# A four-layer graph attention kernel: which sources a target tile takes whole, and how many gather buffers it has

## The chip, the cores and the metric

The kernel runs on one core of one Trainium2 chip, in one launch. The metric is device time in microseconds (us). Three runs of the kernel before gave a median of 1810.38 us, from 1797.26 to 1814.76; the execution that the profile shows took 1796.08 us, and its span from the first to the last instruction is 1794.3 us. The engines are called as the profile calls them: PE multiplies matrices (PEld is its weight load), DVE works on vectors, ACT evaluates functions, POOL (GpSimd) here mostly issues gathers, and SP issues the other transfers.

## The reference

`x` is 4096 x 256 in float32 and `adj` is 4096 x 4096 with entries 0 and 1. An edge between nodes i and j is drawn with a probability proportional to 1/sqrt((1+i)(1+j)), so nodes with a low number are hubs and most of the matrix is zero. Four layers follow each other, each of the form `x = x + attention(relu(layernorm(x)), adj)`:

```python
h = jnp.maximum(_layernorm(x, axis=-1), 0.0)
g = h @ W                                      # projection
e = leaky_relu((g @ a1)[:, None] + (g @ a2)[None, :], 0.2)
att = softmax(where(adj > 0, e, -large), axis=1)
x = x + act(att @ g)
...
```

Layer 0 has one head of 256 and a bias, layer 1 one head and an elu at the end, layer 2 four heads of 64, and layer 3 two attentions over the same mask (the softmax of e and of -e), each with a projection of its own, and an elu. A row of `adj` is a target, a column is a source: each target sums over the sources it has an edge to.

## The kernel before, in words

**Tiles and steps.** The 4096 nodes are 32 tiles of 128, and 8 blocks of four tiles. A *step* is the work of one source tile for a unit of targets. DVE forms the weights `s_p` (the exponential of the leaky relu is a maximum of two products, times the mask; L1032), and PE multiplies them with the sources' projected rows and adds into PSUM (L1068 for layers 0, 1 and 3; L1093 for layer 2, with the operands the other way round). ACT makes the weights of two of the four heads of layer 2 (L1018) before DVE multiplies them with the mask (L1041).

**Two kinds of units.** A *dense* unit holds a block of four target tiles and goes over all 32 source tiles. `DENSE = (4, 2, 1, 1)` blocks are treated so in layers 0 to 3. All other target tiles are *listed*, each a unit of its own: it takes the first `DP` source tiles whole, and of the rest only those sources that have an edge to at least one of its 128 targets. These are gathered, 128 rows at a time, by an indirect transfer on POOL (`s_gg`, L1228) from a table of projected rows in memory, through a list of indices `idx_T`. `CAPS[T]` is the number of such gathers of target tile T. A listed tile therefore has `DP + CAPS[T]` steps. Where the lists do not fit into `CAPS`, a flag is set and a dense version of all layers runs afterwards. Before, `DP` is 4.

**Where whole sources lie.** The projected rows of the first `DP` tiles stay on chip (`L.pre`), and so do their masks (`mpre`). The rows of the other tiles go to the table, and dense units of layers 1 to 3 read them back in chunks of four tiles (`s_gs`, with the mask chunk `s_ms`) on the SP queue, three chunk buffers deep. In layer 0 all projected rows stay on chip (`g`).

**The lists and masks.** During layer 0 the adjacency is loaded in int32, turned into bytes (L1322), written to memory chunk by chunk (L1324), and reduced to "which source has an edge to this tile" (`seen`, L1329). `list_sources` turns that into indices: prefix sums, one-hot matrices on DVE (L875) and 28 small matmuls per target tile on PE (L900). The byte masks of the listed sources are gathered as well (`mlist`, L928), once, and kept for all layers; those of target tiles 4 to 15 come along with a layer's first gathers and are copied to `mlist` by ACT (L1240).

**Order.** Instructions of POOL stay in the order in which the program writes them; the other engines' order comes from a scheduler. `run` fetches a step six steps before it is multiplied, so a gather's place on POOL is fixed there. In layer 0 one or two listed steps follow each dense step from dense step 40 on, and one mask gather is issued per dense step. In layer 1, 16 dense steps stand alone at the start and the other 48 are spread over 24 listed tiles; in layer 2, 36 of 128 (one per head and source tile) stand alone and the rest is spread over 14 of 28 tiles; in layer 3, 16 of 64 stand alone and the rest is spread over 28 tiles. Gathers of a layer can start when all its table rows are written. In layers 1 to 3 the gathers share a pool of 9 buffers (`gat`), so POOL is at most 9 gathers ahead of the steps that use them; layer 0 has its own 7.

Of the kernel before, what the change touches and what calls it, by code (L numbers as in the profile page):

```python
# [9 lines left out]
F16 = mybir.dt.float16  # L10
# [7 lines left out]
P = 128  # L18
# [434 lines left out]

DP = CH
JT = NT - DP
TS0 = IT
DENSE = (4, 2, 1, 1)

ORDER = (None, (0, 4, 1, 5, 2, 6, 3, 7), (0, 4, 5, 6, 7, 2, 1, 3), (0, 2, 3, 4, 5, 6, 7, 1))
LISTED0 = 40
CAPS = (25, 17, 15, 13, 12, 11, 11, 10, 10, 9, 9, 9, 8, 8, 8, 8) + (8,) + (7,) * 7 + (6,) * 8
MAXCAP = max(CAPS[TS0:])
OFFS = [sum(CAPS[TS0:T]) for T in range(NT + 1)]
NLIST = OFFS[NT]
# [13 lines left out]
def list_layers(ctx: ExitStack, tc: tile.TileContext, a: dict, out: bass.AP, flag):  # L480
# [305 lines left out]

    def list_constants(pool):

        place = pool.tile([P, P, JT // 2], F16, name="place")
        nc.gpsimd.iota(  # L790
            place, pattern=[[1, P], [0, JT // 2]], base=0, channel_multiplier=0, allow_small_or_imprecise_dtypes=True
        )
        lists = pool.tile([P, MAXCAP, JT * IT], F16, name="lists")
        nc.gpsimd.iota(
            lists,
            pattern=[[1, MAXCAP], [0, JT * IT]],
            base=0,
            channel_multiplier=0,
            allow_small_or_imprecise_dtypes=True,
        )  # L800

        code = pool.tile([P, JT * IT], F16, name="code")
        n = (NT // 2 - DP) * IT
        for part, tiles, base in ((code[:, 0:n], NT // 2 - DP, DP * P - HALF), (code[:, n:], NT // 2, 1)):
            nc.gpsimd.iota(
                part,
                pattern=[[CH * P, tiles // CH], [1, CH], [0, IT]],
                base=base,
                channel_multiplier=CH,
                allow_small_or_imprecise_dtypes=True,  # L810
            )
        sums = []
        for k in range(2):
            t = pool.tile([P, NT // 2 + JT, IT], F32, name=f"sums_{k}")
            nc.gpsimd.memset(t[:, 0 : NT // 2, :], 0.0)
            sums.append(t)
        return place, lists, code, sums

    def list_sources(ib, seen, pool, consts):

        n = JT * IT
        place, lists, code, sums = consts
        half = JT // 2
        used = pool.tile([P, JT, IT], F16, name=f"used_{ib}", tag="used")
        nc.vector.tensor_scalar(used, seen, 0.0, None, op0=ALU.is_gt)
        yield 4.0
# [44 lines left out]

        def one_hot(T, j):

            first = pool.tile([P, P, half], F16, name=f"first_{T}_{j}", tag="first", bufs=2)
            nc.vector.tensor_tensor(  # L875
                first,
                place,
                lof[:, T % IT, j : j + half].unsqueeze(1).to_broadcast([P, P, half]),
                op=ALU.is_equal,
            )  # L880
            return first


        ahead = [(ib * IT + t, j) for t in range(IT) for j in (0, half)]
        firsts = [one_hot(*ahead[0])]
        yield 4.0
        for t in range(IT):
            T = ib * IT + t
            cap = CAPS[T]
            ps = None  # L890
            for j in range(JT):
                if j % half == 0:
                    first = firsts.pop()
                    ahead.pop(0)
                    if ahead:
                        firsts.append(one_hot(*ahead[0]))
                    yield
                if ps is None:
                    ps = ps_mm.tile([P, MAXCAP], F32, name=f"idx_ps_{T}", tag="mm")
                nc.tensor.matmul(  # L900
                    ps[:, 0:cap],
                    lhsT=first[:, :, j % half],
                    rhs=val[:, 0:cap, j * IT + t],
                    start=(j == 0),
                    stop=(j == JT - 1),
                )
                if j % 7 == 6:
                    yield
            idx = keep.tile([P, cap], I32, name=f"idx_{T}", tag=f"idx_{T}")
            nc.vector.tensor_scalar(idx, ps[:, 0:cap], float(HALF), None, op0=ALU.add)  # L910
            index[T] = idx
            yield
# [278 lines left out]
    def run(plan):  # L1191

        n = len(plan)
        for p in range(n + LEAD[3]):
            if p + 4 < n and plan[p + 4][1] == 0 and plan[p + 4][0].is_ready():
                plan[p + 4][0].prepare()
            for lead, stage in zip(LEAD, (Unit.fetch, Unit.begin, Unit.weigh, Unit.multiply)):
                if 0 <= p - lead < n:
                    stage(*plan[p - lead])
            if p >= LEAD[3]:  # L1200
                u = plan[p - LEAD[3]][0]
                clock[0] += u.cost
                pump(posts, u.rates[0], width=2)
                pump(lists_q, u.rates[1])
                gather_masks(u.rates[2])


    def listed_sources(L, T, pool):
# [36 lines left out]
    with ExitStack() as phase:  # L1245
# [65 lines left out]
        def mask_chunk(ib, c):  # L1311

            load()
            if ib == 0:
                behind(c)
            m = (
                mpre[:, :, ib * IB : (ib + 1) * IB]
                if c == 0
                else mpool.tile([P, CH, IB], U8, name=f"s_m_{ib}_{c}", tag="m")
            )  # L1320
            for h, raw in enumerate(loaded[ib, c]):
                nc.vector.tensor_scalar(m[:, h * half : (h + 1) * half, :], raw, 0.0, None, op0=ALU.is_gt)  # L1322
            if c > 0 or ib in MASKS_IN:
                nc.sync.dma_start(mask_rows(ib, c * CH), m)  # L1324
            if ib > 0:
                if c == 0:
                    seen[ib] = lists_p.tile([P, JT, IT], F32, name=f"seen_{ib}", tag="seen", bufs=4)
                else:
                    nc.vector.tensor_reduce(  # L1329
                        seen[ib][:, (c - 1) * CH : c * CH, :].rearrange("p j t -> p (j t)"),  # L1330
                        m.rearrange("p j i -> p (j i)")
                        .bitcast(I32)
                        .rearrange("p (t w) -> p t w", w=P // 4),
                        AX.X,
                        ALU.max,
                    )
                if c == NCH - 1:
                    push(lists_q, list_sources(ib, seen[ib], lists_p, consts))
            return m
# [52 lines left out]


    late = ctx.enter_context(tc.tile_pool(name="s_late", bufs=1))
    gat = ctx.enter_context(tc.tile_pool(name="s_gather", bufs=9))
    stream = ctx.enter_context(tc.tile_pool(name="s_stream", bufs=3))
    for l in (2, 3):
        L = weights(l, late, late, nc.sync)
# [11 lines left out]
    for l in (1, 2, 3):  # L1410
        L = layers[l]

        def all_sources(L, T0, nt, heads, per):


            held = {}
            n = L.part
            cols = slice(heads[0] * n, (heads[-1] + 1) * n)
            w = slice(T0 * P, (T0 + nt) * P)

            def get(i):
                jt, k = divmod(i, per)
                jt = ORDER[L.l][jt // CH] * CH + jt % CH
                mine = heads[k : k + 1] if per > 1 else heads
                if jt < DP:
                    ensure(lambda: L.ready[jt])
                    return mine, [L.pre[:, jt, h * n : (h + 1) * n] for h in mine], mpre[:, jt, w]
                if jt % CH == 0 and k == 0:
                    ensure(lambda: all(L.ready[jt : jt + CH]))
                    gt = stream.tile(  # L1430
# [112 lines left out]
```

## Time and profile before

| | before |
|---|---|
| median of 3 runs | 1810.38 us |
| span of the profiled execution | 1794.3 us |
| ACT busy | 631.0 us (35%) |
| gathers of rows `s_gg` / of masks `mlist` | 715 / 105 |
| layer 0 ends (last addition to x, L1122) | 520.6 us |
| layer 1 ends (L1140) | 852.0 us |
| layer 2 ends (L1160) | 1370.0 us |
| layer 3 ends (L1182) | 1783.3 us |

Each float32 matmul stands in the records as two instructions (1430 of them for the 715 gathered steps of one matmul each), and a group's busy time, not its mean, counts what it really occupied. [...] Idle time of an engine counts only in a stage in which another engine waits for it. For POOL, idle time that ends with a PE or DVE instruction is a wait for a free buffer; a gap of 0.30 us, put down to "issue" or to whatever semaphore came last, stands ahead of every gather.

### The profile page before, as it was taken

To read this page: it belongs to the slowest core of one execution; us is meant where nothing else is said; L and a number is where in the kernel's file an instruction comes from. 1 tells how busy PE (TensorE), PEld (TensorE's weight loads), DVE (VectorE), ACT (ScalarE), POOL (GpSimd) and SP (SyncE) were. 2 spreads that over 40 slices of the span, in tenths; PEclk is the share of its full clock that TensorE was granted. 3 is DMA by queue.
4 is the path that set the end of the run, shared out by engine and by line. 5 is a ranking of instruction groups with operands and counts; after the bars stand their busy time and mean duration, and the time that the engine had idled before them with its cause. 6 is when DMAs were issued, how large, how long until landed. Compare 5 with 4: busy or idle time off the path is not lost.

```text
span 1794.3 us, 29158 instructions
## 1 busy us (share of the span) xinstructions
PE 1660.2 (93%) x9268; PEld 1384.3 (77%) x9268; DVE 1319.1 (74%) x3908; ACT 631.0 (35%) x1915; POOL 960.5 (54%) x930
## 2 busy tenths in 40 slices
PE   6998899799889999888999999988889999999997
PEld 4886777678778778676577878788888888888876
DVE  6787899777744676556788888877785566777755
ACT  5630010020120232333467666788884011111101
POOL 8836666646535656553353444444561666655453
PEclk9999999999879999989999999999999999999999
DMA  7888778853244444543233332323342665666553
GB/s 258 301 299 281 242 244 251 264 143 110 60 135 138 134 117 134 147 132 106 82 94 86 90 90 81 98 82 83 99 116 75 197 208 175 183 180 178 160 165 107
DMA packets 152237, 274.70 MB, mean 153 GB/s; under 512 B 21423, under 2 KB 75340, under 8 KB 152076
## 3 DMA queue, kind: packets, MB, share of 16 engines
q0 software_dynamic: 45584, 130.39, 26.8%
q1 hardware_dynamic: 105656, 141.83, 24.2%
q8 instruction: 77, 1.26, 0.3%
q14 instruction: 84, 0.69, 0.1%
q10 hardware_dynamic: 836, 0.53, 0.1%
HBM read 231.76 MB, written 40.90 MB: 152 GB/s over the span
## 4 chain that ended last, share of the span: by engine, by line
PE 78%; DVE 8%; issue 4%; DMA 3%; POOL 3%; ACT 2%; another core or an unknown queue 2%; SPq 0%; POOLq 0%; DVEq 0%; ACTq 0%
PE s_acc L1068 44%; PE s_accm L1093 20%; PE s_pj L748 8%; DVE s_p L1032 3%; PE idx_ps L900 2%; PE s_tp L716 2%; PE s_sT L966 2%; DMA s_gg<-table,idx 1%; DMA s_raw<-in_adjT 1%; ACT s_p L1018 1%; DVE s_m L1322 1%; POOL s_z L702 1%; POOL s_gg L1228 1%; DVE s_p L1041 0%
## 5 line engine op out<-in xcount | busy, mean ns | idle before, releaser
L1228 POOL DMA_INDIRECT s_gg<-table,idx x715 | 757.9, 1060 | 733.5 <-PE s_acc L1068 228.6
L1032 DVE SCALAR_TENSOR_TENSOR s_p<-s_grow,s_gg,mlist 128x128 f32<-128x128 f32 x994 | 310.1, 346 | 143.0 <-PE s_acc L1068 85.9
L1068 PE MATMUL s_acc<-s_gg,s_p 128*128 128x257 f32 x1430 | 353.8, 390 | 9.9 <-DVE s_p L1032 7.8
L1068 PEld LDWEIGHTS s_acc<-s_gg,s_p 128*128 128x128 f32 x1430 | 270.5, 194 | 53.6 <-DVE s_p L1032 12.6
L1068 PE MATMUL s_acc<-g,s_p 128*128 128x257 f32 x1152 | 292.5, 397 | 14.2 <-DVE s_p L1032 5.3
L1068 PEld LDWEIGHTS s_acc<-g,s_p 128*128 128x128 f32 x1152 | 220.0, 198 | 49.7 <-issue 12.3
L1032 DVE SCALAR_TENSOR_TENSOR s_p<-s_grow,pre,mpre 128x128 f32<-128x128 f32 (+1 forms) x576 | 189.2, 369 | 49.4 <-PE s_acc L1068 30.5
L1093 PE MATMUL s_accm<-s_p,s_gg 128*65 128x128 f32 x1744 | 204.7, 273 | 1.7 <-issue 1.6
L1068 PE MATMUL s_acc<-s_gs,s_p 128*128 128x257 f32 x896 | 203.6, 380 | 0.0
L1032 DVE SCALAR_TENSOR_TENSOR s_p<-s_grow,s_gs,s_ms 128x512 f32<-128x512 f32 x224 | 161.9, 748 | 50.7 <-PE s_accm L1093 24.7
L748 PE MATMUL s_pj<-s_w,s_hT 128*128 128x259 f32 (+3 forms) x640 | 175.9, 417 | 24.9 <-ACT s_hT L718 9.5
L1093 PEld LDWEIGHTS s_accm<-s_p,s_gg 128*65 128x65 f32 x1744 | 193.2, 138 | 5.3 <-issue 2.8
L1018 ACT ACTIVATE s_p<-s_grow,s_minus,s_gg 128x128 f32<-128x128 f32 x436 | 186.7, 485 | 25.9 <-PE s_accm L1093 15.0
L1068 PE MATMUL s_acc<-pre,s_p 128*128 128x257 f32 x768 | 184.0, 384 | 5.5 <-ACT s_y L1179 3.5
L1068 PEld LDWEIGHTS s_acc<-s_gs,s_p 128*128 128x128 f32 x896 | 169.4, 190 | 24.7 <-issue 0.6
L972 ACT ACTIVATE s_grow<-s_sT 128x256 f32<-128x256 f32 (+2 forms) x136 | 46.8, 367 | 379.3 <-PE s_sT L966 260.9
L748 PEld LDWEIGHTS s_pj<-s_w,s_hT 128*128 128x128 f32 x640 | 126.3, 205 | 56.4 <-ACT s_hT L718 14.2
L1068 PEld LDWEIGHTS s_acc<-pre,s_p 128*128 128x128 f32 x768 | 144.5, 192 | 28.4 <-ACT s_y L1179 3.9
L928 POOL DMA_INDIRECT mlist<-mask_t,idx x105 | 122.1, 1162 | 65.1 <-issue 30.0
L1093 PE MATMUL s_accm<-s_p,pre 128*65 128x128 f32 (+1 forms) x928 | 122.2, 286 | 2.6 <-issue 2.5
L1093 PEld LDWEIGHTS s_accm<-s_p,pre 128*65 128x65 f32 x928 | 105.1, 139 | 21.0 <-issue 18.3
L1018 ACT ACTIVATE s_p<-s_grow,s_minus,pre 128x128 f32<-128x128 f32 x224 | 95.0, 485 | 23.2 <-issue 18.9
(126 smaller groups left out, 1743.5 us busy)
## 6 DMA issues: line engine op xcount, KB each, us to landing
s_raw<-in_adjT SPq DMA_DIRECT2D x128, 512.0 KB
s_gs<-table SPq DMA_DIRECT2D x28, 516.0 KB
s_gg<-table,idx POOLq DMA_INDIRECT x715
mask_t<-s_m SPq DMA_DIRECT2D x35, 256.0 KB
table<-s_g SPq DMA_DIRECT2D x28, 258.0 KB
s_ms<-mask_t SPq DMA_DIRECT2D x28, 256.0 KB
table<-s_m SPq DMA_DIRECT2D x21, 256.0 KB
table<-g SPq DMA_DIRECT2D x8, 516.0 KB
```

Of the source, the lines that this page charges most:

```text
L702: (nc.gpsimd if L.l == 0 else nc.vector).tensor_scalar(z, x[:, T, :], mv[:, k, 0:1], 0.0, op0=ALU.subtract, op1=ALU.max)
L716: nc.tensor.transpose(tp[:, c, :], zs[k][:, c * P : (c + 1) * P], ident)
L748: nc.tensor.matmul(ps, lhsT=hT[:, c, :], rhs=L.w[:, c, k * (D + 6) : k * (D + 6) + cols], start=(c == 0), stop=(c == 1),)
L900: nc.tensor.matmul(ps[:, 0:cap], lhsT=first[:, :, j % half], rhs=val[:, 0:cap, j * IT + t], start=(j == 0), stop=(j == JT - 1),)
L928: nc.gpsimd.indirect_dma_start(out=mlist[:, OFFS[T] + k, :], out_offset=None, in_=mask_t[T // IT], in_offset=bass.IndirectOffsetOnAxis(ap= ...
L966: nc.tensor.transpose(ps[:, h - h0, it, :], L.s[:, T0 + it, h : h + 1].to_broadcast([P, P]), ident)
L972: nc.scalar.activation(grow[:, h1:h2, :], ps[:, h1 - h0 : h2 - h0].rearrange("p h a b -> p h (a b)"), AF.Exp, scale=scale,)
L1018: nc.scalar.activation(w[:, h, :], u.grow[:, h, :], AF.Relu, scale=g[h][:, n - 1 : n], bias=minus)
L1032: nc.vector.scalar_tensor_tensor(p[:, k, :], u.grow[:, h, :], g[k][:, n - 1 : n], m, op0=ALU.min if L.l == 3 and h == 1 else ALU.max, op1= ...
L1068: nc.tensor.matmul(u.accs[it][h], lhsT=p[:, k, it * P : (it + 1) * P], rhs=g[k][:, 0:n], start=first, stop=last,)
L1093: nc.tensor.matmul(u.regions[h], lhsT=g[k][:, 0 : DH + 1], rhs=p[:, k, :],  start=first and (u.nt > 1 or h == 0), stop=last, skip_group_ch ...
L1228: nc.gpsimd.indirect_dma_start(out=wide, out_offset=None, in_=L.table, in_offset=bass.IndirectOffsetOnAxis(ap=index[T][:, k : k + 1], axis=0),
```

## The change

Only source tile 0 is still taken whole; tiles 1 to 3 join the lists. A source tile taken whole costs a step, whether its sources have edges to these 128 targets or not; a listed one costs only its share of the gathered rows. So `DP` falls from 4 to 1 and `CAPS` rises, and every listed tile has one or two steps fewer and one to three gathers more. `JT`, the number of listed source tiles, goes from 28 to 31, an odd number, so the one-hot matrices come in halves of 16 and 15 tiles. The first chunk of source tiles is now treated as all others: its mask is written to memory and reduced, and its rows and mask are read back by the dense units of layers 1 to 3. The on-chip copies `L.pre` and `mpre` shrink to a quarter, and the room goes to 17 gather buffers in place of 9. In layer 0, every fourth dense step issues two mask gathers instead of one.

```diff
-DP = CH
+DP = 1
 JT = NT - DP
+HALFT = (JT + 1) // 2
...
-CAPS = (25, 17, 15, 13, 12, 11, 11, 10, 10, 9, 9, 9, 8, 8, 8, 8) + (8,) + (7,) * 7 + (6,) * 8
+CAPS = (28, 20, 17, 16, 14, 13, 13, 12, 12, 11, 11) + (10,) * 4 + (9,) * 5 + (8,) * 8 + (7,) * 4
...
-                gather_masks(u.rates[2])
+                gather_masks(u.rates[2] and u.rates[2] + (plan[p - LEAD[3]][1] % 4 == 3))
...
-            m = (
-                mpre[:, :, ib * IB : (ib + 1) * IB]
-                if c == 0
-                else mpool.tile([P, CH, IB], U8, name=f"s_m_{ib}_{c}", tag="m")
-            )
+            m = mpool.tile([P, CH, IB], U8, name=f"s_m_{ib}_{c}", tag="m")
...
-            if c > 0 or ib in MASKS_IN:
-                nc.sync.dma_start(mask_rows(ib, c * CH), m)
+            nc.sync.dma_start(mask_rows(ib, c * CH), m)
             if ib > 0:
                 if c == 0:
                     seen[ib] = lists_p.tile([P, JT, IT], F32, name=f"seen_{ib}", tag="seen", bufs=4)
-                else:
-                    nc.vector.tensor_reduce(
...
+                    nc.scalar.copy(mpre[:, :, ib * IB : (ib + 1) * IB], m[:, 0:DP, :])
+                j0 = DP if c == 0 else 0
+                nc.vector.tensor_reduce(
...
-    gat = ctx.enter_context(tc.tile_pool(name="s_gather", bufs=9))
+    gat = ctx.enter_context(tc.tile_pool(name="s_gather", bufs=17))
...
-                if jt < DP:
-                    ensure(lambda: L.ready[jt])
-                    return mine, [L.pre[:, jt, h * n : (h + 1) * n] for h in mine], mpre[:, jt, w]
                 if jt % CH == 0 and k == 0:
```

## The prediction

> **What bounds the kernel now.** I read the page first, then the busy time of each engine in stretches that follow the layers, then POOL's waits, then single gathers in time order.
>
> ```profile
> PE 1660.2 (93%) x9268; PEld 1384.3 (77%) x9268; DVE 1319.1 (74%) x3908; ACT 631.0 (35%) x1915; POOL 960.5 (54%) x930
> ...
> L1228 POOL DMA_INDIRECT s_gg<-table,idx x715 | 757.9, 1060 | 733.5 <-PE s_acc L1068 228.6
> ```
>
> PE looks like the bound and POOL half idle. By stretch (layer 0 to 537; layer 1 to 852, its target tiles 16 to 31 to 716, then 8 to 15; layer 2 to 1390; then layer 3), each column being busy us with the number of instructions:
>
> ```profile
> core 0: us, PE busy (x) PEld busy (x) DVE busy (x) ACT busy (x) POOL busy (x), PEclk, DMA share, GB/s
> 121.00:235.00 114.00, 98.09 (x575) 80.81 (x573) 96.65 (x229) 11.05 (x40) 80.58 (x64) 0.98 0.85 270
> ...
> 537.00:716.00 179.00, 167.58 (x786) 141.01 (x785) 114.61 (x362) 39.99 (x143) 105.78 (x105) 0.99 0.46 130
> 716.00:852.00 136.00, 116.37 (x484) 92.04 (x483) 79.53 (x238) 43.45 (x158) 68.10 (x69) 0.92 0.45 129
> 852.00:1146.00 294.00, 289.22 (x1839) 213.37 (x1838) 255.94 (x748) 187.89 (x498) 131.93 (x121) 0.99 0.32 87
> 1146.00:1390.00 244.00, 222.13 (x1726) 206.79 (x1725) 186.69 (x638) 189.68 (x557) 101.51 (x99) 0.99 0.33 93
> 1390.00:1707.00 317.00, 316.00 (x1479) 274.76 (x1478) 218.91 (x706) 38.27 (x98) 189.45 (x180) 1.00 0.62 183
> ```
>
> The first part of layer 2 and most of layer 3 are PE's almost without a gap (289 of 294, 316 of 317); the second part of layer 2 has PE at 222 of 244. Layers 0 and 1 are not: PE has 6 to 14% of idle time, and no other engine is full either. POOL's own rhythm, in layer 3:
>
> ```profile
> 1570.16 0.95 POOL L1228 DMA_INDIRECT s_gg<-table,idx  x1 [0.30 <-PE s_acc L1068]
> 1571.41 0.95 POOL L1228 DMA_INDIRECT s_gg<-table,idx  x1 [0.30 <-PE s_acc L1068]
> ...
> 1581.76 1.34 POOL L1228 DMA_INDIRECT s_gg<-table,idx  x1 [4.38 <-PE s_acc L1068]
> ```
>
> A gather costs POOL 0.95 us plus a gap of 0.30 us which no view counts as busy. So the price is a *pitch*: mean busy plus 0.30. From the stretches: layer 0, 80.58/64 = 1.26, so 1.56 in the one shown, and 1.45 over the whole layer from 121 on (213 instructions, 244.2 us); layer 1, 105.78/105 and 68.10/69, so 1.30; layer 2, 1.39 and 1.33; layer 3, 1.35. With that, POOL is occupied for 180 x 1.35 = 243 of 317 us in layer 3, not 189, and the waits of 4.38 us are its slack: a free buffer, released by PE.
>
> For PE's price of a step I take runs in the chain of waits:
>
> ```profile
> 41.92 3.04 PE s_acc L1068 x14
> ...
> 966.37 2.62 PE s_accm L1093 x24
> ```
>
> Seven matmuls of 257 columns in 3.04 us are 0.434 each; twelve of layer 2 in 2.62 are 0.218 each, 0.873 for a step of four heads.
>
> [...]
>
> **The change, part by part.** Steps of listed tiles, from the sums of CAPS: layer 0 (tiles 16 to 31) 169 to 144, layer 1 (8 to 31) 270 to 235, layers 2 and 3 (4 to 31) 330 to 291 each. Gathers of rows: 105 to 128, 174 to 211, 218 to 263, 218 to 263, together 150 more; mask gathers 105 to 128. Counting sources with the reference's inputs, all lists fit, so the dense fallback stays out.
>
> PE loses 25 x 0.434 = 10.9 us in layer 0, 35 x 0.434 = 15.2 in layer 1, 39 x 0.873 = 34.1 in layer 2, 78 x 0.434 = 33.9 in layer 3 (two attentions). It gains 28 x 3 = 84 list matmuls at 0.07 (14 take 0.98 us), 5.9 us, in layer 0. Net 88 us less.
>
> DVE loses 216 weights of 346 ns and 39 of 417, 91 us, of which only 8.7 in layer 0. There it gains nearly 15 us: the one-hots (60.8 us) grow by 124/112, the two list products (11.8 us) by 1736/1344, and seven more reductions take at most 0.68 each. ACT loses 78 x 0.485 = 38 us and gains 22 mask copies (6.4) and seven copies of one mask tile (at most 0.6 each: a copy of 512 columns takes 577 ns); layer 2's weights hide them. SP writes five more mask chunks of 256 KB in layer 0, against 67 MB of adjacency: nothing that the 0.85 DMA share there would show.
>
> POOL gains 173 gathers, about 235 us. What that means, by layer:
>
> Layer 0. From the first mask gather (121.0) to the last row gather (514.4) are 393 us, of which 210 x 1.45 = 305 are occupied. After: 256 x 1.45 = 371. It fits, with 22 us to spare in a queue in fixed order, where a gather that waits for an index or a buffer holds up all behind it, and PE's listed steps after those. PE's tail after the last dense step gets shorter (33 listed steps were left at 470; the order of the changed kernel leaves about 15). Between -15 and +30; I take +5.
>
> Layer 1. Rows are gathered from 537 on. 211 x 1.30 = 274, so the last is issued at 811 at the earliest; add 6 for waits and the 23 that lie between the last gather (829.3) and the end now: 840 against 852, -12. PE alone would allow -15, and more if 17 buffers close the bubbles of tiles 8 to 15, but POOL's sum does not.
>
> Layer 2. POOL needs 135 x 1.39 = 188 of 294 us and 128 x 1.33 = 170 of 244. It stays below PE, so PE's 34.1 come through: -33.
>
> Layer 3. POOL: 263 x 1.345 = 354 from 1390, 1744; plus 4 for waits and the 22 from the last gather (1772.6) to the end: 1770 against 1794, -24. PE alone would allow -34. The 17 buffers matter here: they let POOL use the 16 dense steps at the start (28 us) to get 17 gathers ahead, 23 us of the 28; with 9, it would have had 12.
>
> The added wait: each of the five dense units of layers 1 to 3 now loads chunk 0, where it had `pre` on chip. At the start of layer 1 that load waits on SP for the last gathers of layer 0; behind it on SP are the mask chunk, later chunks and the last row stores. PE first needs it some 5 us later (now transposes and a projection fill 522 to 526). From 0 to 8 us; I take 2, inside layer 1's 6. In layers 2 and 3 chunk 0 has long been written and a chunk buffer is free early, hidden behind the preceding listed tiles.
>
> Sum: 5 - 12 - 33 - 24 = -64 us of 1794.3, 3.6%; on the median of 1810.4, 1746.
>
> **The rivals.** *PE stays the bound everywhere.* For it: POOL's waits for PE releases are 228.6 + 128.4 us, and gathers without interference take 1.25. Then 88 us go, and about 10 more from bubbles in tiles 8 to 15 of layer 1, where ACT waits 61.9 us for gathers to land. Against it: the sums 274 and 354 above. 1712.
>
> *Layer 0 eats the gain.* POOL's queue and DVE (97 of 114 us busy) are both close to full there; +30 in layer 0, -5 in layer 1, -20 and -10 after: 1805, no change.
>
> *POOL's waits don't shrink.* Its time between the first and the last gather of a layer, less the occupied part, is 393 - 305 = 88 us in layer 0, 292 - 226 = 66 in layer 1 and 383 - 293 = 90 in layer 3. If half of that is latency rather than slack, the gathers of layer 0 end at 121 + 371 + 44 = 536 against 514 (+22, and up to +20 more for dense steps that stall behind them), layer 1 at 537 + 274 + 33 + 23 = 867 (+15), and layer 3 at 1390 + 354 + 45 + 22 = 1811 (+17); with -33 in layer 2 that is +41, so 1851, slower. Against it: in layer 3 the waits come once per tile right after seven gathers back to back, which is the picture of a full buffer pool, not of latency.
>
> **How the numbers follow.** POOL takes over layers 1 and 3 (1746): 0.54. PE stays the bound (1712): 0.26. Layer 0 eats the gain (1805): 0.10. Waits stay (1851): 0.10. The range from 1700 to 1790 leaves out the last and most of the third. Faster by over 1% (below 1792): the first two and a fifth of the third, some of the first lost to a larger layer 0, 0.82; within 1%: 0.09; slower: 0.09.
>
> **What would show it.** 865 row gathers with a pitch near 1.3; POOL's waits for PE nearly gone in layers 1 and 3, and PE's share falling from 316 of 317 there; layer 2 shorter by 33 with PE still full; the last layer-0 gather still near 515. The prediction is wrong if POOL's pitch moves (a tenth of a us is 26 us in layer 3 alone), if layer 0 grows by tens of us, or if PE waits for chunk 0 at layer starts.

## The result, and the profile after

The changed kernel took 1899.17 us (median of 4 runs, 1894.10 to 1903.07) against 1803.82 us for the kernel before, measured beside it (4 runs): 1.052 times as long, with an interval of 1.045 to 1.060. I had forecast 1746 us and given slower a chance of 0.09.

One thing about the numbers has to be said first, because it came out of the experiments and runs through all of them. On two chips of the runs below the kernel before takes 1700 us, on four it takes 1782 to 1798 us, and the first measurement resembles these four. I call them 1700-us chips and 1790-us chips. No chip is on record at two times, so it isn't shown whether the difference belongs to the chip itself or to something that held there at that time. Every ratio of the experiments compares runs on one chip.

Page of the changed kernel, first measurement: engines, and the group of row gathers.

```profile
PE 1643.3 (87%) x8764; PEld 1343.3 (71%) x8764; DVE 1263.3 (67%) x3660; ACT 606.9 (32%) x1866; POOL 1141.8 (60%) x1104
...
L1233 POOL DMA_INDIRECT s_gg<-table,idx x865 | 914.5, 1057 | 636.7 <-PE s_acc L1073 187.0
```

There are 865 gathers, and one costs POOL what it did before (mean 1057 ns, before 1060). But POOL, which was to be full, has 637 us of idle time left before them. PE executes 504 instructions fewer and its share falls from 93 to 87%, in a longer span. By stretch (the first is that of before; then layer 1, layer 2, and 317 us of layer 3 from its first gather on, as before):

```profile
core 0: us, PE busy (x) PEld busy (x) DVE busy (x) ACT busy (x) POOL busy (x), PEclk, DMA share, GB/s
121.00:235.00 114.00, 93.30 (x523) 74.46 (x522) 84.60 (x184) 11.04 (x40) 82.82 (x68) 0.87 0.75 236
552.00:925.00 373.00, 304.96 (x1301) 244.77 (x1300) 193.31 (x594) 94.15 (x342) 210.42 (x211) 0.89 0.49 138
925.00:1437.00 512.00, 467.36 (x3162) 377.49 (x3161) 402.36 (x1251) 342.85 (x968) 277.45 (x263) 0.97 0.39 106
1456.00:1773.00 317.00, 270.46 (x1182) 227.07 (x1181) 172.35 (x558) 33.31 (x85) 214.24 (x201) 0.92 0.67 199
```

In layer 3 PE executes 1182 instructions in 317 us where it executed 1479, and POOL issues 201 gathers where I expected 317/1.345 = 236. Neither is full, and the granted clock (the first number after POOL) is down from 1.00 to 0.92. POOL's rhythm there:

```profile
1561.27 0.95 POOL L1233 DMA_INDIRECT s_gg<-table,idx  x1 [0.30 <-issue]
1564.29 0.94 POOL L1233 DMA_INDIRECT s_gg<-table,idx  x1 [2.07 <-remote]
...
1569.64 0.94 POOL L1233 DMA_INDIRECT s_gg<-table,idx  x1 [2.90 <-DVE s_p L1037]
1571.35 0.94 POOL L1233 DMA_INDIRECT s_gg<-table,idx  x1 [0.77 <-PE s_acc L1073]
```

The 0.95 and the 0.30 are unchanged, but between them stand waits of 0.8 to 2.9 us, as they would for a free buffer of the 17. Who holds the buffers? The waits of PE's weight loads and of DVE, and a piece of the chain that ended last:

```profile
PEld s_acc L1073 <- issue: 89.9, 59, 10.1
```

```profile
DVE s_p L1037 <- PE s_acc L1073: 154.7, 130, 10.5
```

```profile
1493.31 10.42 PE s_acc L1073 x48
1503.72 9.74 issue
1513.46 2.24 PE s_acc L1073 x2
```

DVE waits up to 10.5 us for PE to give back a weight buffer (before: 3.7 at most), and PE's records show up to 10.1 us in which it waits for nothing that the profile names (before: 17.9 us in all, 3.0 at most). So PE is late without being busy. Who ended a wait is inferred from records of completions, and in this trace a good part of these is missing (numbers further down), so "issue" and "remote" can stand for a release that isn't on record.

Layers, in us, from the end of one to the end of the next. The end is that of the last addition to x in layers 0 and 2, of the last reciprocal in layer 1 (L1140 as further up; its last addition comes 5.6 us later), and of the last subtraction in layer 3 (L1184), so up to 2.4 us later than the starts given further up. In the changed kernel these lines are numbered 5 higher:

| | layer 0 | 1 | 2 | 3 |
|---|---|---|---|---|
| before, first measurement | 521 | 331 | 519 | 415 |
| changed, first measurement | 552 | 373 | 512 | 453 |
| before, a second 1790-us chip | 521 | 332 | 513 | 413 |
| changed, the same chip | 557 | 380 | 512 | 453 |
| before, a 1700-us chip | 481 | 313 | 490 | 405 |
| changed, the same chip | 515 | 335 | 458 | 380 |

### The profile page after: what moved, and what is told of

Same layout as the page of the kernel before. It is cut to its first block, busy times and chain, and to the rows that moved or that the text cites. A ratio compares the mean times of both kernels' runs of the same rounds, so it can differ in the third digit from the quotient of the medians.

```text
span 1898.6 us, 28332 instructions
## 1 busy us (share of the span) xinstructions
PE 1643.3 (87%) x8764; PEld 1343.3 (71%) x8764; DVE 1263.3 (67%) x3660; ACT 606.9 (32%) x1866; POOL 1141.8 (60%) x1104
## 4 chain that ended last, share of the span: by engine, by line
PE 73%; issue 9%; DVE 7%; DMA 4%; ACT 3%; another core or an unknown queue 3%; POOL 1%; SPq 0%; POOLq 0%; ACTq 0%; DVEq 0%
PE s_acc L1073 40%; PE s_accm L1098 19%; PE s_pj L749 8%; DMA s_gg<-table,idx 2%; DVE s_p L1037 2%; PE idx_ps L905 2%; PE s_tp L717 2%; PE s_sT L971 2%; DVE s_m L1323 1%; DMA s_raw<-in_adjT 1%; ACT s_p L1023 1%; DVE first L880 1%; PE s_oT L1160 1%; POOL s_gg L1233 0%
## 5 line engine op out<-in xcount | busy, mean ns | idle before, releaser
L1233 POOL DMA_INDIRECT s_gg<-table,idx x865 | 914.5, 1057 | 636.7 <-PE s_acc L1073 187.0
L1037 DVE SCALAR_TENSOR_TENSOR s_p<-s_grow,s_gg,mlist 128x128 f32<-128x128 f32 x1204 | 373.5, 344 | 228.0 <-PE s_acc L1073 98.2
L1073 PE MATMUL s_acc<-s_gg,s_p 128*128 128x257 f32 x1730 | 452.7, 406 | 35.7 <-issue 14.9
L1073 PEld LDWEIGHTS s_acc<-s_gg,s_p 128*128 128x128 f32 x1730 | 339.8, 204 | 99.9 <-issue 30.3
L1098 PE MATMUL s_accm<-s_p,s_gg 128*65 128x128 f32 x2104 | 258.4, 278 | 15.4 <-issue 15.3
L1073 PEld LDWEIGHTS s_acc<-g,s_p 128*128 128x128 f32 x1056 | 209.2, 205 | 57.6 <-issue 14.2
L1098 PE MATMUL s_accm<-s_p,s_gs 128*65 128x512 f32 x256 | 115.9, 592 | 0.0
L1037 DVE SCALAR_TENSOR_TENSOR s_p<-s_grow,g,s_m 128x512 f32<-128x512 f32 x128 | 97.8, 772 | 8.6 <-PE s_acc L1073 4.1
L1323 DVE TENSOR_SCALAR s_m<-s_raw 128x1024 uint8<-128x1024 int32 x128 | 90.7, 721 | 8.9 <-DMA s_raw<-in_adjT 8.4
L1046 DVE SCALAR_TENSOR_TENSOR s_p<-s_p,mlist 128x256 f32<-128x256 f32 x211 | 87.7, 416 | 12.0 <-ACT s_p L1023 9.7
L717 PE MATMUL s_tp<-s_ident,s_z 128*128 128x128 f32 x256 | 49.6, 302 | 49.0 <-ACT s_grow L977 15.6
L1184 ACT ACTIVATE s_y<-s_acc,s_rz 128x256 f32<-128x256 f32 x32 | 14.8, 473 | 240.9 <-issue 109.0
```

Of the source, the lines that this page charges most:

```text
L717: nc.tensor.transpose(tp[:, c, :], zs[k][:, c * P : (c + 1) * P], ident)
L1037: nc.vector.scalar_tensor_tensor(p[:, k, :], u.grow[:, h, :], g[k][:, n - 1 : n], m, op0=ALU.min if L.l == 3 and h == 1 else ALU.max, op1= ...
L1046: nc.vector.scalar_tensor_tensor(p[:, own:, :], p[:, own:, :], 1.0, m.unsqueeze(1).to_broadcast([P, u.nact, w]), op0=ALU.add, op1=ALU.mult,)
L1073: nc.tensor.matmul(u.accs[it][h], lhsT=p[:, k, it * P : (it + 1) * P], rhs=g[k][:, 0:n], start=first, stop=last,)
L1098: nc.tensor.matmul(u.regions[h], lhsT=g[k][:, 0 : DH + 1], rhs=p[:, k, :],  start=first and (u.nt > 1 or h == 0), stop=last, skip_group_ch ...
L1233: nc.gpsimd.indirect_dma_start(out=wide, out_offset=None, in_=L.table, in_offset=bass.IndirectOffsetOnAxis(ap=index[T][:, k : k + 1], axis=0),
```

## The experiments

**First set: is it thin work for PE, the buffers, or the mask rate?** My first theory was that a PE with gaps between gathered steps is granted a slower clock. The recorded clock fits it, without showing that the gaps are the cause: in the first measurement 298 us at half speed in the changed kernel (mean clock 0.922), 111 before (0.970), in multiples of 3.413 us but for one cut off by the end.

Three steps per listed tile left out of the kernel before, in layers 1 to 3:

```diff
         def get(i):
+            if L.l > 0 and i > 0:
+                i += DP - 1
...
-                L, T, 1, DP + CAPS[T], listed_sources(L, T, gat), ...
+                L, T, 1, 1 + CAPS[T], listed_sources(L, T, gat), ...
```

> The kernel before, but in layers 1 to 3 every listed target tile leaves out its steps for source tiles 1 to 3 (so those sources are missing from its sums); no gather is added. That takes 72 steps of 0.434 us from layer 1, 84 of 0.873 from layer 2 and 84 of 0.868 from layer 3: 177 us of PE. If the sums of my prediction hold (PE's price per step is fixed, POOL has room with its 218 gathers), about 1630 us. If a PE that waits between gathered steps is granted a slower clock (clock theory), the clock falls from 0.97 to 0.94 or less and a good part of the 177 us is lost: 1700 us or more.

Source tile 0 taken four times in the changed kernel:

```diff
         def get(i):
+            if L.l > 0:
+                i = max(i - 3, 0)
...
-                L, T, 1, DP + CAPS[T], listed_sources(L, T, gat), ...
+                L, T, 1, DP + 3 + CAPS[T], listed_sources(L, T, gat), ...
```

> The changed kernel, but in layers 1 to 3 every listed target tile takes source tile 0 four times instead of once (so it counts four times in its sums): 177 us more work for PE, DVE as in the kernel before, and no gather more or less. If PE's work simply adds up where it was late, about 2050 us, and at least 1980. Clock theory: PE idles less between gathered steps, the granted clock goes from 0.92 to 0.96 or more, and the added work costs little: 1890 to 1930 us. If the 150 added gathers themselves are what is slow (traffic, POOL), the time is set by them and hardly moves either, but the clock stays near 0.92.

Nine buffers:

```diff
-    gat = ctx.enter_context(tc.tile_pool(name="s_gather", bufs=17))
+    gat = ctx.enter_context(tc.tile_pool(name="s_gather", bufs=9))
```

> The changed kernel with 9 gather buffers instead of 17. If deep runs of gathers are the harm (they collide with DVE's or PE's work or with other transfers), the time goes back towards 1800 us. If the 17 buffers help as I forecast, it gets slower, to about 1920. Clock theory: about 1900, within 25 either way, since the buffers don't alter how much PE has to do between gathers.

The old mask rate:

```diff
-                gather_masks(u.rates[2] and u.rates[2] + (plan[p - LEAD[3]][1] % 4 == 3))
+                gather_masks(u.rates[2])
```

> The changed kernel with one mask gather per dense step of layer 0, as before. If the faster mask rate is what makes layer 0 longer by 28 us, about 1870 us; if the listing itself is, 1899 within 10.

Measured, all on one chip, on which the kernel before took 1700.36 us:

| | us | ratio, interval | layers 0 to 3 |
|---|---|---|---|
| three steps fewer, before | 1570.98 | 0.924, 0.922 to 0.926 | 484, 300, 432, 344 |
| tile 0 four times, changed | 1847.86 | 1.087, 1.085 to 1.090 | 510, 350, 530, 445 |
| 9 buffers, changed | 1740.62 | 1.023, 1.020 to 1.026 | 516, 330, 489, 393 |
| old mask rate, changed | 1698.32 | 0.999, 0.998 to 1.000 | 512, 333, 458, 382 |

The surprise was the kernel before itself, 1700 us, and with it that the change without its faster mask rate costs nothing here. Of 177 us of PE work, 129 are saved when it is left out, and some 150 are paid when it is added (1847.86 against 1698.32 with the old mask rate): on this chip most of PE's work comes through in the time, the clock stays at 0.97 to 0.98, and the clock theory is not needed. The mask rate does not explain layer 0 (512 us; with it, in the third set, 515). The 17 buffers help, by 42 us against the run with the old mask rate, 31 of them in layer 2 and 11 in layer 3.

**Second and third set: the same two kernels elsewhere.**

> The kernel before, unchanged, for its trace on the chip on which the others of this set run. In the first set it took 1700 us, against 1804 us when the change was measured. If chips differ in how they run the same program, the trace shows where: the PE groups' waits put down to issue, the granted clock, or the transfers.

> The changed kernel, unchanged. With one mask gather per dense step fewer it took 0.999 of the kernel before in the first set. If the 5% of the first measurement belongs to the change, the ratio is 1.05 here too; if it belongs to the chip or its state (waits of PE put down to issue, up to 10 us, which no kernel of the first set shows), it is 1.00, within 0.01.

> The kernel before, unchanged, for its trace beside the three others of this set. It took 1700 us in the first set and 1798 us in the second; either is possible here, and the trace (PE's waits put down to issue, PE's completions at a regular pace or not) should go with the time.

> The changed kernel, unchanged. If the loss belongs to chips on which PE's completions come late while gathers run: about 1.06 of the kernel before where that one takes 1800 us, and 1.00 (0.99 to 1.01) where it takes 1700 us. If the loss belongs to the change alone, 1.05 or more in either case.

On a chip where the kernel before took 1797.99 us, the unchanged copy gave 1.000 (0.997 to 1.002) and the changed kernel 1907.05 us, 1.063 (1.057 to 1.068). On one where it took 1699.54 us: 1.000 (0.999 to 1.001) and 1698.14 us, 0.998 (0.996 to 1.000). So the loss belongs to the change *on a kind of chip*. The stretches of the kernel before on the 1700-us chip (layers 1 and 2, and 317 us of layer 3):

```profile
481.00:794.00 313.00, 292.61 (x1326) 244.45 (x1327) 203.26 (x620) 87.34 (x315) 172.18 (x174) 0.96 0.49 141
794.00:1284.00 490.00, 483.69 (x3474) 402.18 (x3473) 431.36 (x1367) 375.96 (x1038) 237.22 (x218) 1.00 0.34 95
1303.00:1620.00 317.00, 317.00 (x1486) 276.24 (x1485) 227.46 (x709) 39.35 (x100) 182.15 (x182) 1.00 0.62 184
```

And of the changed kernel there, with POOL's rhythm in layer 3:

```profile
515.00:850.00 335.00, 287.99 (x1300) 237.90 (x1298) 194.65 (x590) 94.03 (x341) 209.49 (x211) 0.92 0.53 153
850.00:1309.00 459.00, 450.85 (x3164) 366.85 (x3163) 398.43 (x1254) 343.79 (x970) 284.32 (x263) 1.00 0.42 118
1327.00:1644.00 317.00, 312.64 (x1449) 268.96 (x1448) 215.99 (x692) 40.99 (x104) 243.41 (x241) 0.99 0.77 236
```

```profile
1502.78 0.95 POOL L1233 DMA_INDIRECT s_gg<-table,idx  x1 [0.30 <-DVE s_p L1037]
1504.03 0.95 POOL L1233 DMA_INDIRECT s_gg<-table,idx  x1 [0.30 <-PE s_acc L1073]
1505.29 0.95 POOL L1233 DMA_INDIRECT s_gg<-table,idx  x1 [0.30 <-DMA s_gg<-table,idx]
```

That is the picture I had drawn: 241 gathers in 317 us, in all of layer 3 no gap above 0.5 us (the kernel before: 27 of them, 96 us), a mean pitch of 1.315. DVE now waits for gathers, not for PE:

```profile
DVE s_p L1037 <- DMA s_gg<-table,idx: 110.3, 96, 5.1
DVE s_p L1037 <- PE s_acc L1073: 85.3, 171, 2.9
```

Four more facts from the traces of the two kinds. DVE's weights for the lone dense steps of the changed kernel, without or nearly without gathers, take the same time on both: from the first to the last, 18.6 and 18.7 us in layer 1, 36.4 and 36.4 in layer 2, 23.1 and 23.1 in layer 3. On the 1790-us chip PE's completions come irregularly while gathers run: 498 of 2088 on record follow the one before within 0.1 us, where a step takes 0.434; on the 1700-us chip none of 2478. And on the 1790-us chip a good part of the completions is missing from the record (2267 of DVE's, where the 1700-us chip has 3387). Instructions are on record in full on both. Packets of the transfers are too, and by them the gathered rows are not late on the 1790-us chip: from the end of POOL's interval to the last packet of a gather it is 2.2 us on average there and 2.3 us on the other.

**Layers 0 and 1, which are longer on both kinds.** As many gathers as before, with all the rest of the change (the last sources of each list are left out):

```diff
-        for k in range(CAPS[T])
+        for k in range(CAPB[T])       # CAPS of the kernel before
...
-            u = Unit(L0, T, 1, DP + CAPS[T], ...)     # and in layers 1 to 3
+            u = Unit(L0, T, 1, DP + CAPB[T], ...)
```

> The changed kernel (tiles 1 to 3 listed, 17 buffers, chunk 0 read back), but each listed tile makes only as many gathers of rows and of masks as before, 715 and 105, in all layers; the last 39 to 128 or so of its listed sources are left out of the sums, so its steps are those of the kernel before less three. If the 173 added gathers are what the change costs, layer 0 is as long as before and the time is below that of the kernel before with three steps left out in layers 1 to 3 (ratio 0.924): 0.90 to 0.92. If it is the added lists, the mask writes or the readback of chunk 0, layer 0 stays some 28 us longer and the ratio is 0.935 or more.

> The changed kernel with only as many gathers per tile as before (715 and 105; the last sources of each list left out), as in the second set, where the kernel before took 1798 us and this 0.962 of it. Where the kernel before takes 1700 us: the added gathers and their steps account for the loss in layers 0 and 1 if layer 0 comes back from 515 to 480 to 492 us and layer 1 from 335 to 300 to 308; the ratio is then 0.90 to 0.92. If lists, mask writes or chunk 0 cost as much, layer 0 is 500 or more.

Measured on two 1790-us chips: 1725.07 us, 0.962 (0.956 to 0.968), layers 533, 340, 461, 378; and 1702.01 us, 0.955 (0.949 to 0.961), layers 527, 334, 456, 371. Both are above the 0.935 that I had named, but I had derived it from a 1700-us chip, so the ratio alone says little. Layer 0 says more: it stays 6 to 12 us above the 521 of the kernel before although its PE has 48 steps fewer (21 us). But 20 to 24 us of the longer layer 0 and 40 of layer 1 go with the added gathers and their steps. No run of this kernel is on a 1700-us chip.

Masks of tiles 16 to 19 moved into layer 0's table, ahead of its rows:

```diff
-MASKS_IN = {1: (2, False), 2: (1, False), 3: (1, True)}
+MASKS_IN = {1: (2, False), 2: (1, False), 3: (1, True), 4: (0, False)}
```

> The changed kernel, but the masks of target tiles 16 to 19 lie in layer 0's table ahead of the rows and come along with layer 0's row gathers, as layers 1 and 2 do it for other tiles: 36 of the 128 mask gathers are gone, and ACT copies 36 masks more. If POOL's queue is what makes layer 0 some 28 us longer than before, 36 x 1.45 = 52 us leave that queue and layer 0 gets 15 to 30 us shorter; if it is the lists' work on DVE and PE or the mask writes, layer 0 stays within 5 us.

1708.55 us, 1.005 (1.003 to 1.006), on a 1700-us chip: slower than the changed kernel, layer 0 is 526 us, not shorter. It took 36 gathers out of POOL's queue and put another wait in:

```profile
ACT mlist L1246 <- DMA s_gg<-table,idx: 185.6, 101, 16.6
```

Before these copies ACT is idle for 185.6 us in all, until the gather of the mask has landed, at most 16.6 us at a time; in the changed kernel it is 89.8 us, at most 14.2. So the run neither proves nor refutes that POOL's queue sets layer 0. The traces of the third set say more. The conversion of the adjacency to masks goes along with the dense steps, from the first chunk to the last; here for before, and then for the changed kernel:

```profile
L1322 DVE TENSOR_SCALAR s_m<-s_raw x112: 669/687/1212, 28.1 to 411.1; 128x1024 uint8<-128x1024 int32 x112
```

```profile
L1323 DVE TENSOR_SCALAR s_m<-s_raw x128: 672/686/1210, 7.6 to 459.7; 128x1024 uint8<-128x1024 int32 x128
```

The dense part of layer 0 ends 49 us later (x112 and x128, because 16 conversions of before go to `mpre`). What POOL has done from 121 until then, in the same order:

```profile
121.00:411.00 290.00, 274.95 (x1713) 232.71 (x1712) 264.75 (x652) 39.78 (x145) 197.24 (x167) 0.99 0.80 246
```

```profile
121.00:460.00 339.00, 308.59 (x1836) 257.64 (x1836) 285.38 (x680) 45.13 (x163) 256.96 (x222) 0.94 0.75 228
```

POOL has issued 167 gathers in one case and 222 in the other (77 and 108 of rows). The order puts one or two *steps* of listed tiles behind each dense step. Before, 4 of the 10 to 12 steps of a tile need no gather, now one of 8 to 10, so the same 130 listed steps ahead of the last dense one need 115 gathers in place of 81. With the 0.30 ahead of each, POOL is occupied for 324 of 339 us, where it was 247 of 290, and DVE's waits for gathered rows between 110 and 540 us rise from 11.8 to 32.4: I read this as POOL pacing the dense part. The tail behind the last conversion gets shorter, as I had said, 54 us instead of 69, but it had hidden something. The indices of the last block (tiles 12 to 15) are made in it; first and last start, before and after:

```profile
L910 DVE TENSOR_SCALAR idx<-idx_ps x28: 123/160/170, 120.1 to 458.7; 128x6 int32<-128x6 f32 x8, 128x7 int32<-128x7 f32 x7, 128x8 int32<-128x8 f32 x5, 128x9 int32<-128x9 f32 x3
```

```profile
L915 DVE TENSOR_SCALAR idx<-idx_ps x28: 124/165/173, 126.5 to 518.3; 128x8 int32<-128x8 f32 x8, 128x9 int32<-128x9 f32 x5, 128x10 int32<-128x10 f32 x4, 128x7 int32<-128x7 f32 x4
```

They were ready 22 us before layer 0's end (481) and now come 3 us after it (515), with DVE, PE and ACT busy on them and on the projections that stand behind, so the first weight of layer 1 comes 10.4 us after the end of layer 0, before 3.2:

```profile
525.32 6.29 DVE L1037 SCALAR_TENSOR_TENSOR s_p<-s_grow,s_gs,s_ms 128x512 f32<-128x512 f32 x9 [1.72 <-ACT s_grow L977]
```

It waits for the exponentials of the targets (ACT), not for the chunk 0 that is now read back. No run changed this order alone, so that POOL paces layer 0, and what the tail hid, is read from the traces and not shown by an experiment.

Gathers that nothing reads, in the kernel before, as many as the change adds in layers 1 to 3 (127):

```diff
+                if L.l > 0 and k % 2 and k // 2 < CAPA[T] - CAPS[T]:   # CAPA: CAPS of the changed kernel
+                    idle = idle_p.tile([P, P], F32, ...)
+                    nc.gpsimd.indirect_dma_start(out=idle, in_=L.table, ...)
```

> The kernel before with 37, 45 and 45 more row gathers in layers 1, 2 and 3 (as many as the change adds there), of 512 B a row, into two buffers that nothing reads, and no step more or less. By my sums POOL has room for them in all three layers: no change, within 10 us. If gathers slow PE down by being there (late completions), 20 to 60 us more where the kernel before takes 1800 us, and no change where it takes 1700 us. If POOL's waits in the kernel before are latency rather than slack, 20 us or more on any chip.

On the 1700-us chip: 1733.84 us, 1.020 (1.018 to 1.021), layers 481, 336, 498, 409. 34 us for work that nothing waits for, 23 of them in layer 1, where 211 gathers then take 298 us (275 for 174 before, 281 for 211 in the changed kernel with its 17 buffers). POOL's waits in layer 1 were not all room.

**What makes the 1790-us chips lose more.** Zeros multiplied by zeros, to fill PE's gaps:

```diff
+                if L.l > 0 and u.nt == 1 and i >= DP:      # layers 1 and 3
+                    nc.tensor.matmul(u.accs[0][heads[0]][:, 0:P], lhsT=zeros, rhs=zeros, start=False, stop=False)
```

> The changed kernel with one more matmul of zeros by zeros (128 columns, about 0.217 us) ahead of each gathered step of layers 1 and 3, 474 in all, 103 us of PE work that changes no sum and waits for nothing new. Where the kernel before takes 1800 us and the changed one 1907 us: if PE is slowed there because it has gaps between gathered steps, the added work fills them, the recorded clock rises from 0.93 to 0.95 or more and the time stays at or falls below 1907 us (ratio 1.06 or less); if PE's work just adds up, 1960 us or more. Where the kernel before takes 1700 us: PE has about 40 us of gaps in these two layers, so 1740 to 1790 us.

> The changed kernel with source tile 0 taken four times instead of once in layers 1 to 3 (it counts four times in the sums): 177 us more of PE work. In the first set it took 1.087 of the kernel before, 150 us more than the changed kernel. Where the kernel before takes 1800 us: if gaps make PE slow there, 1900 to 1940 us, ratio 1.08 or less and a clock above the changed kernel's 0.93; if the work adds up as elsewhere, 2040 us, ratio 1.13 or more. Where the kernel before takes 1700 us it repeats 1.087.

The zero matmuls gave 1913.50 us, 1.071 (1.064 to 1.077) with the clock at 0.944; tile 0 four times 2000.34 us, 1.121 (1.115 to 1.127) at 0.95. Against the changed kernel's 1.052 and 1.063 on two such chips that is 15 to 33 us for 103 us of work, and 104 to 122 us for 177. Both lie between the two theories. PE has gaps there that swallow most of the first, and the clock rises a little (from 0.922 and 0.928 in the changed kernel), but filling them gives no time back.

More weight buffers, with 14 gather buffers to make room, and the control:

```diff
-    work = ctx.enter_context(tc.tile_pool(name="s_work", bufs=7))
+    works[True] = ctx.enter_context(tc.tile_pool(name="s_work1", bufs=10))   # 7 in the control; layer 0 keeps 7
...
-    gat = ctx.enter_context(tc.tile_pool(name="s_gather", bufs=17))
+    gat = ctx.enter_context(tc.tile_pool(name="s_gather", bufs=14))
```

> The changed kernel with 14 gather buffers instead of 17, and with 7 buffers for the weights as before, those of layers 1 to 3 in a pool of their own: the control for the next one. About 1.00 to 1.01 of the kernel before where that one takes 1700 us, 1.055 to 1.075 where it takes 1790 us.

> The same with 10 instead of 7 buffers for the weights s_p in layers 1 to 3, so DVE can be three steps further ahead of PE. Where the kernel before takes 1790 us: if the loss there is in the handshake (PE's completions reach DVE late, DVE waits up to 10 us for a weight buffer, PE then waits for weights), the ratio falls by 0.015 or more against the control; if PE itself or the gathers are slow there, it stays within 0.007. Where the kernel before takes 1700 us, within 0.007 of the control, since completions come at a regular pace.

1878.54 us, 1.054 (1.047 to 1.061), and 1882.44 us, 1.055 (1.049 to 1.061), on one chip. So three more buffers between DVE and PE change nothing. The handshake itself does not fall with that, because the traces show it to be slow. Two of DVE's weights from the first measurement, in the 9.74 us of the chain above in which PE executes nothing:

```profile
1505.65 0.61 DVE L1037 SCALAR_TENSOR_TENSOR s_p<-s_grow,s_gg,mlist 128x128 f32<-128x128 f32 x2 [2.94 <-remote]
1509.20 0.61 DVE L1037 SCALAR_TENSOR_TENSOR s_p<-s_grow,s_gg,mlist 128x128 f32<-128x128 f32 x2 [2.94 <-remote]
```

Both wait for PE's semaphore alone; their rows had landed by 1497.8, and PE's last matmul stands in the records as over at 1503.72. So PE's completions reach DVE late. To see how late, I assigned the buffers to the steps in order. On the 1700-us chip all 83 waits of DVE for PE alone, at gathered steps of layer 3, end within 0.04 us of the moment at which the rows had landed and the matmul that frees the buffer was over. In the first measurement the 76 such waits end up to 5.0 us after it, 59 us in all; in the kernel before it is 33 us, at most 2.9. The ends of PE's records are modelled, so whether the matmul itself was late or only the word of it can't be told. Why three more buffers don't bridge such delays is not known either.

The idle gathers once more, and half the bytes in layer 3:

> The kernel before with 37, 45 and 45 row gathers more in layers 1, 2 and 3 that nothing reads, as in the third set, where it took 1.020 of the kernel before (34 us, 23 of them in layer 1, 8 in layer 2, 4 in layer 3) on a chip where that one takes 1700 us. Where it takes 1790 us: if gathers slow PE down there by being under way, the ratio is 1.035 or more and layer 3 loses more than 20 us; if they only queue on POOL as elsewhere, 1.02 within 0.007 and layer 3 within 10 us.

```diff
-                wide = pool.tile([P, GW[L.l] + more], F32, ...)
+                gw = L.part if L.l == 3 else GW[L.l]
+                wide = pool.tile([P, gw + more], F32, ...)
```

> The changed kernel, whose gathers in layer 3 fetch only the first of the two projections of a row, 1032 of 2064 B, which then serves both attentions (so the second is computed with the wrong rows in listed tiles); the same number of gathers, weights and matmuls. Where the kernel before takes 1790 us: if the traffic of the gathers makes layer 3 slow (453 us against 380), it gets 25 us or more shorter; if their number does, it stays within 10 us. Where the kernel before takes 1700 us, POOL sets layer 3's pace at 1.32 us a gather and it stays within 8 us of 380.

Idle gathers on a 1790-us chip: 1902.37 us, 1.065 (1.058 to 1.073), layers 517, 369, 552, 464. This settles most of it for layers 1 to 3. The kernel before, with not a step less and not a list longer, becomes as slow as the changed kernel by 127 gathers whose rows nobody reads. The price of one is 116/127 = 0.91 us of the whole time, where it is 34/127 = 0.27 us on a 1700-us chip. Its page (the idle gathers cost POOL little more than the others, whose mean is 1049 ns) and 317 us of its layer 3:

```profile
L1238 POOL DMA_INDIRECT idle<-table,idx x127 | 140.7, 1108 | 38.7 <-issue 31.1
```

```profile
1456.00:1773.00 317.00, 287.73 (x1261) 239.63 (x1260) 183.76 (x603) 32.35 (x82) 206.43 (x190) 0.95 0.56 165
```

and the same stretch of the kernel before on such a chip:

```profile
1385.00:1702.00 317.00, 316.54 (x1481) 275.30 (x1481) 219.85 (x709) 38.48 (x98) 190.07 (x181) 1.00 0.62 183
```

The number of gathers in the stretch hardly rises, 190 with the idle ones against 181, POOL is not full (206.43 + 190 x 0.30 = 263 of 317 us), and PE falls from 1481 instructions to 1261.

Half rows: 1895.43 us, 1.059 (1.049 to 1.069); layer 3 is 441 us instead of 453. Half the bytes bring back 12 of the 73 us that separate the two kinds of chip there, a little over the 10 that I had allowed for no effect and well below the 25 for traffic; and the 453 are from other chips. So it goes mainly with the number of gathers and little with their bytes.

## Why the prediction was wrong, step by step

**PE's saving** (layer 2: -33). The sum was right on the 1700-us chip, where layer 2 is shorter by 32 us; on the 1790-us chips it is 2 to 7 us. But even on the 1700-us kind it took the buffers: with 9 of them layer 2 lasts 489 us, one less than before. I had counted on the 17 buffers in layer 3 alone, where they were worth 11.

**Layer 3** (-24, POOL takes over). On the 1700-us chip: -26, with POOL's pitch at 1.315 (I had 1.345) and hardly a wait for a buffer. There the likeliest case happened as drawn, with less of a head start: the first gather of layer 3 starts 18.8 us after layer 2's end, when PE has 8 us of the lone dense steps left, which is room for 6 gathers and not for 17. In the first measurement it is +38.

**Layer 1** (-12). POOL's part was right: 211 gathers were to take 274 us plus 6, and took 281 on the 1700-us chip. But the time from the last gather to the end, kept at 23, is 32, the gathers start 22 us after layer 0 and not 16, and before, they had taken 275 there, not 292. So it is +22 instead of -12. Why the tail is 9 us longer was not followed up. The 7 us at the start are the index work that layer 0 no longer hides.

**Layer 0** (+5). "It fits, with 22 us to spare" failed, and "PE's tail after the last dense step gets shorter" was counted as a gain only. The occupied time of 371 us was right (369). But I held it against the whole layer and not against the part before the last dense step, in which most of it falls by the order of the steps; on the 1700-us chip it would not even have fitted the whole, since from 121 to the last row gather of the kernel before there are 352 us. Layer 0 grew by 34 us on the 1700-us chip and by 31 to 35 on the others. The rival "Waits stay" had the last gather at 536; it came at 541.

**The step that failed.** For layers 1 to 3 it is one that I never wrote down. I charged a gather to POOL's queue alone, and a matmul always at its full price; for layer 2 this reads "It stays below PE, so PE's 34.1 come through", and layers 1 and 3 are summed in the same way. On a 1790-us chip a gather that nothing reads costs about 0.9 us of the whole time although POOL has time for it, 116 us for the 127 of layers 1 to 3, while the 83 us of PE work that the change saves there are worth only the share that the experiment with tile 0 shows, 0.59 to 0.69. With 31 us for layer 0 that is 116 - 53 + 31 = 94 us; measured were 95 in the first run and 109 in the second. This accounting is an estimate from other kernels' runs, not a measurement of its terms in this one.

**The rivals.** "POOL's waits don't shrink" (1851, 0.10) ended on the right side, for a reason close to its own in layers 0 and 1 and for a wrong one in layer 3, where the waits vanish on one kind of chip and on the other go with PE's late completions. The wait for chunk 0, which I put at 2 us, is not what the first weight of layer 1 waits for.

**Could the profile of before have told?** In part. Its clock of 0.97 (0.985 on the 1700-us chip), PE's waits put down to "issue" (17.9 us for the weight loads of `s_acc`; on the 1700-us chip such a wait is not among the seven largest, which go down to 6.2) and DVE's waits of up to 3.7 us for PE (2.8 there) are marks of the 1790-us kind. It could not tell that they grow with the number of gathers.

**What stays open.** Why PE's completions come late on some chips while gathers run, and how much of the loss in layers 1 and 2 this is. The recorded half clock explains less than half: with the idle gathers it rises from 102 to 205 us, which is worth at most half the difference, 51 of 116 us. A candidate, a guess of mine that nothing here shows, is the recording itself: the 1790-us chip's trace lacks completions (2267 of DVE's on record against 3387), and the loss goes with the number of gathers. But every run here is recorded, so no run separates the chip from its recording. Of the versions that compute the whole reference, none beats the kernel before by more than 0.2% on either kind of chip.

## What to carry to other kernels

Price an asynchronous transfer by what a useless copy of it costs the whole kernel, not by the time its issuing engine is busy; 127 unread gathers told more than any sum. Idle time of an engine in a fixed order is room only where the order puts the new work: hold the added work against each part of a layer (here the dense part of layer 0), and ask what a tail hides before counting its shortening as a gain. Where an engine waits for another, hold the end of the wait against the work that should end it: here up to 5.0 us lay between them. And measure on more than one chip before explaining a few per cent, since the same change was 0.998 on one and 1.06 on another.

## What was not expected of the hardware

- The same kernel takes 1700 us on some chips and 1782 to 1798 on others; DVE's weights for lone dense steps are equal to 0.1 us on both.
- In layer 3 of the changed kernel DVE's waits for PE alone end within 0.04 us of the recorded end of the matmul that frees a buffer on a 1700-us chip, and up to 5.0 us after it on a 1790-us chip.
- A gather of 128 rows costs POOL as much in layer 3, with 2064 B a row, as in layer 1, with 1032 and where masks come along some more (medians 0.949 and 0.949 us before, 0.946 and 0.946 in the changed kernel, first measurement), and a gap of 0.30 us; the idle gathers, of 512 B a row, have means of 1.043 and 1.108 us beside 1.046 and 1.049 for the other row gathers of their runs; and halving the bytes in layer 3 moved that layer by 12 of 453 us.
- 17 gather buffers instead of 9 are worth 2.5% of the changed kernel on a 1700-us chip; from 17 to 14 no loss is seen on a 1790-us chip (1.054 against 1.052 and 1.063).
